# Graph attention on one core: one gathered tile in six steps, row by row through SyncE

## The chip, the cores and the metric

One NeuronCore of one Trainium2 chip. The metric is the device time of one execution in microseconds: 1808.31 us as the median of three runs before the change (1808.1 to 1808.62).

Engine names are those of the profile: PE (TensorE matmuls) and PEld (its weight loads), DVE (VectorE), ACT (ScalarE), POOL (GpSimd), SP (SyncE, which here only issues DMAs). A name with a q (SPq, POOLq) is that engine's instruction queue.

## What is computed

One layer of attention over a graph of 6250 nodes with 64 channels (4 heads of 16) and 206250 edges that are sorted by destination. For every edge: a score per head from the source's key, the destination's query and the edge's own projected values; then the sum of the sources' values, weighted by the scores, at each destination; then a residual and a layer norm.

```python
Qh, Kh, Vh = x @ Wq.T + bq, x @ Wk.T + bk, x @ Wv.T + bv      # each as (n, 4, 16)
Ee = edge_attr @ We.T + be
score = (Kh[src] * Qh[dst] * (1 / sqrt(16)) * Ee).sum(-1)
score = exp(clip(score, -5, 5))
msg = Vh[src] * score[..., None]
wV = segment_sum(msg, dst, num_segments=n)
out = layernorm(x + wV)
```

## The kernel before

**Preparation.** Keys and values of all nodes are computed once and written to a table in HBM, `kv_tab`, one row of 128 floats (512 B) per node; queries go to `q3_tab`. All sources and destinations lie in SBUF as `src_i` and `dst_i`, one column per tile.

**Tiles, groups, steps.** The edges are cut into 1612 tiles of 128 edges, 8 tiles make a group, and 2 groups a step; the last eight groups are steps of their own, 105 steps in all (`NS`). The loop over steps at L671 is unrolled in the program and its order is written by hand: each engine runs its instructions in the order in which that loop calls them, and waits for others by semaphores.

**Keys and values of an edge's source** come in two ways.
- `gather_kv` (L389): GpSimd issues one indirect DMA per tile (L391), which fetches 128 rows of `kv_tab` into one column of the step's buffer. There are `KVB = 5` such buffers (`kvs`, 128 x 16 x 128 floats), and `gather(s + 4)` (L507, called at L704) is issued in step s, so gathers may run up to four steps ahead.
- For the last two tiles of a step, in steps 6 to 96, the row of x is picked on TensorE by one-hot matrices that VectorE makes (`sources`, `hots` L470, `picks` L480), and keys and values are computed from it (`picked_kv`, L499), whereupon ScalarE writes them to the last two columns of the buffer. So in these steps GpSimd gathers 14 tiles of 16.

**A step's chain.** VectorE multiplies keys, queries and edge values (`products`: L565 waits for the step's gathers, then L566), sums by head (L572), ScalarE takes the exponential (L575), VectorE makes the message (L582); ScalarE and TensorE split it into three bf16 parts (L585, L593, L595), and TensorE sums by destination (L601). Interleaved with these are the next step's edge values (`edges`, L377 and L380), its queries (L558), and one-hot rows (ScalarE L535, L540).

**SP's queue.** In the order of the loop SP issues: the edges of two steps ahead (`fetch_edges`, L157, 512 KB), the two query windows of two steps ahead (`fetch_queries`, L171; their start rows come from registers that L165 loads from SBUF, 8 at a time), and at the end of some steps rows of x for a closed block (`close`, L636) and finished rows of the output (`norm`, L654). SP works in order and stops at a transfer whose buffer isn't free yet: L157 and L171 wait for TensorE to be done with the buffer's last use, L636 and L654 for VectorE. The built program counts the completion of SP's DMAs on eight semaphores in turn, so a DMA also waits, where that is not yet known to be past, for the one issued eight before it.

Of the kernel before, what the change touches and what calls it, by code (L numbers as in the profile page):

```python
# [7 lines left out]
F32 = mybir.dt.float32  # L8
BF16 = mybir.dt.bfloat16
I32 = mybir.dt.int32  # L10
AF = mybir.ActivationFunctionType
# [3 lines left out]
P = 128  # L15
N = 6250
C = 64
# [3 lines left out]
T = -(-E // P)  # L21
G = 8
NG = -(-T // G)

STEPS = [(g, 2) for g in range(0, NG - 8, 2)] + [(g, 1) for g in range(NG - 8, NG)]
NS = len(STEPS)
# [12 lines left out]
KVB = 5  # L39
# [10 lines left out]
def tiles_of(g):  # L50
    return min(G, T - g * G)
# [6 lines left out]
def groups_of(s):  # L58
    return range(STEPS[s][0], STEPS[s][0] + STEPS[s][1])
# [7 lines left out]
def picks_in(s):  # L67
    return M0 <= s <= LAST


def about_where(g):
    return STEP * g + g // 32

# [16 lines left out]

@with_exitstack
def tile_gnn(ctx: ExitStack, tc: tile.TileContext, x, xT, wT, bias, beT, weT, eT, src, dst, dst_rows,
             out):
    nc = tc.nc
    consts = ctx.enter_context(tc.tile_pool(name="consts", bufs=1))
    dram = ctx.enter_context(tc.tile_pool(name="dram", bufs=1, space=bass.MemoryType.DRAM))
# [3 lines left out]
    kv_tab = dram.tile([NR, 2 * C], F32, name="kv_tab")  # L100
# [6 lines left out]
    kvs = [consts.tile([P, 2 * G, 2 * C], F32, name=f"kv{i}") for i in range(KVB)]  # L107

    def kv_of(g):

        s = max(s for s in range(NS) if STEPS[s][0] <= g)
        j = (g - STEPS[s][0]) * G
        return kvs[s % KVB][:, j:j + G, :]
# [39 lines left out]
    def fetch_edges(q):  # L153

        lo, hi = q * LG * G // 2, min((q + 1) * LG * G, T) // 2
        et = loads.tile([P, LG * G // 2, P], F32, name="et")
        nc.sync.dma_start(et[:, :hi - lo, :], eT[:, lo:hi, :])  # L157
        for g in range(q * LG, min((q + 1) * LG, NG)):
            ET[g] = et[:, (g % LG) * G // 2:(g % LG + 1) * G // 2, :]

    def fetch_queries(g):

        if g % RG == 0:
            for i in range(2):
                _, vs = nc.values_load_multi_w_load_instructions(  # L165
                    base[i:i + 1, g // 2:(g + RG) // 2], engines=[mybir.EngineType.SP], min_val=0,
                    max_val=N, skip_runtime_bounds_check_because="the least of some destinations")
                for k, v in enumerate(vs):
                    at[g + 2 * k + i] = v
        QW[g] = windows.tile([3 * W, C], BF16, name="qw")  # L170
        nc.sync.dma_start(QW[g], q3_tab[bass.ds(at[g], W), :].rearrange("n (i c) -> (n i) c", i=3))  # L171

    with tc.tile_pool(name="nodes", bufs=1) as nodes, \
# [23 lines left out]
        for i in range(NB // CB):  # L197
            s = slice(i * CB * P, (i + 1) * CB * P)
# [18 lines left out]
        for g in range(XG):  # L217
            for j in range(G):
                nc.gpsimd.indirect_dma_start(
                    out=XS[g][:, j, :], out_offset=None, in_=x[:, :],  # L220
# [138 lines left out]
        for g in range(XG):  # L359
            for h in range(2):  # L360
                tp = npsum.tile([P, 2, P], F32, name="tp", bufs=2)
                for u in range(2):
                    j = 4 * h + 2 * u
# [25 lines left out]
    def gather_kv(g, j):  # L389
        t = g * G + j  # L390
        nc.gpsimd.indirect_dma_start(  # L391
            out=kv_of(g)[:, j, :], out_offset=None, in_=kv_tab[:, :],
            in_offset=bass.IndirectOffsetOnAxis(ap=src_i[:, t:t + 1], axis=0))
# [7 lines left out]
    with tc.If(rv == 0) as branch:  # L401

        with tc.tile_pool(name="work", bufs=2) as work, \
# [45 lines left out]
            def sources(s, i):  # L449

                if picks_in(s):
                    FAR[s, i] = work.tile([P, P], BF16, name="far")
                    nc.scalar.activation(FAR[s, i], row50, AF.Identity,
                                         bias=src_f[:, s - M0, i:i + 1], scale=-1.0)

            def sources_turned(s, i):
                if picks_in(s):
                    nc.tensor.transpose(from_b[i], FAR.pop((s, i)), ident_b)  # L460
# [46 lines left out]
            def gather(s):  # L507
                for g in groups_of(s):
                    for j in range(tiles_of(g)):
                        if not picks_in(s - 2) or g == STEPS[s][0] or j < G - 2:  # L510
                            gather_kv(g, j)


            def spread(g):

                pb = psum.tile([P, G, P], F32, name="pb")
                for b in range(0, tiles_of(g), 4):
                    nc.tensor.matmul(pb[:, b:b + 4, :],  # L518
                                     ident_b[:NR2, g // 2:g // 2 + 1].to_broadcast([NR2, P]),
                                     key_rows[:, g % 2, b * P:(b + 4) * P], start=True, stop=True)  # L520
                return pb
# [8 lines left out]
            def onehot_rows(g, pb):  # L530

                n = tiles_of(g)
                TO[g] = work.tile([3 * W, G, P], BF16, name="to", bufs=4)

                nc.scalar.activation(TO[g][:, :n, :], pb[:3 * W, :n, :], AF.Square,  # L535
                                     bias=minus_row3[:3 * W])

            def onehot_rows_rest(g):
                n = tiles_of(g)
                nc.scalar.activation(TO[g][:, :n, :], TO[g][:, :n, :], AF.Relu, bias=one_p[:3 * W],  # L540
                                     scale=-1.0)
# [55 lines left out]
            def sums(s):  # L597
                n = tiles_in(s)
                PA[s] = pa
                for j in range(n):  # L600
                    nc.tensor.matmul(PA[s], OH[s][:, j, :], M3[s][:, j], start=j == 0, stop=j == n - 1)  # L601
# [45 lines left out]
            def scales(lo, hi):  # L647
                nc.vector.reciprocal(rstd[:, lo:hi], rstd[:, lo:hi])
# [22 lines left out]
            for s in range(NS):  # L671
                more = s + 1 < NS
                for g in groups_of(s):
                    if g % LG == 0 and g + 2 * LG < NG:
                        fetch_edges(g // LG + 2)
                if s + 2 < NS:
                    for g in groups_of(s + 2):
                        fetch_queries(g)
                nexts = list(groups_of(s + 1)) if more else []
                if more:  # L680
                    onehot_rows(nexts[0], spread(nexts[0]))
                    onehot_rows_rest(nexts[0])
                if s:
                    sums(s - 1)
                sources_turned(s, 1)
                sources_turned(s + 1, 0)
                if nexts[1:]:
                    onehot_rows(nexts[1], spread(nexts[1]))
                making = [b for b in range(s * 2 * TB, (s + 1) * 2 * TB, TB) if b < NB]
                if making:  # L690
                    rest = table_parts(making[0])
                prod = products(s)
                picked(s - 1)
                if more:
                    edges(s + 1, 0)
                picks(s, 0, 0)
                score = scores(s, prod)
                if nexts[1:]:
                    onehot_rows_rest(nexts[1])
                if s:  # L700
                    add(s - 1)
                msg = message(s, score)
                if s + KVB - 1 < NS:
                    gather(s + KVB - 1)  # L704
                picked_turned(s - 1)
                if nexts[1:]:
                    edges(s + 1, 1)
                minus(s, msg, 0)
                hots(s, 1, 0)
                picks(s, 0, 1)  # L710
                minus(s, msg, 1)
                picked_kv(s - 1)
                if not more:

                    close(B - 2)
                    spreads(B - 2)
                hots(s, 1, 1)
                picks(s, 1, 0)
                sources(s + 1, 1)
                sources(s + 2, 0)  # L720
                if more:
                    if nexts[0] * G % KEYS == 0:
                        keys(nexts[0] * G)
                    onehot_edges(s + 1)
                    queries(s + 1)
                picks(s, 1, 1)
                hots(s + 1, 0, 0)
                hots(s + 1, 0, 1)
                if more:

                    while closed < B - 2 and due[closed] <= s:
                        close(closed)
                        spreads(closed)
                        closed += 1
                    if closed in BATCHES and closed > scaled:
                        roots(scaled, closed)
                        scales(scaled, closed)
                        scaled = closed
                    for _ in range(3):
                        if normed < scaled:  # L740
                            norm(normed)
                            normed += 1
                for i, b in enumerate(making):
                    if i:
                        rest = table_parts(b)
                    table_parts_rest(b, rest)
# [175 lines left out]
```

## Time and profile before

The profiled execution took 1808.39 us; its span from the first to the last instruction is 1806.6 us.

| engine | busy us | share of the span | instructions |
|---|---|---|---|
| PE | 1641.5 | 91% | 15751 |
| PEld | 1370.4 | 76% | 15751 |
| DVE | 1481.7 | 82% | 1695 |
| ACT | 912.0 | 50% | 1313 |
| POOL | 1351.8 | 75% | 1442 |

SP is not in this table, since instructions that issue DMAs are not counted as busy. The mean granted TensorE clock was 0.95. The DMA queues:

| queue | packets | MB | share of 16 engines |
|---|---|---|---|
| software_dynamic (GpSimd's) | 45760 | 92.76 | 19.6% |
| hardware_dynamic (SP's) | 60204 | 70.01 | 13.5% |

How to read the lines that follow in the prediction:
- A *group* line gives source line, engine, operation, out<-in and the number of instructions; after the bar busy time in us and the mean of one in ns; after the second bar the idle time of the engine just before them, and what ended most of it. "issue" means that the profile shows nothing that the engine waited for.
- A line of the *list of waits* gives who waited, for whom, us in total, how many times, and the longest.
- A line of the *timeline* gives start, duration, engine, source line, operation and shapes, and in brackets the idle time before it and what ended it. A line of the *chain* (the work that ended last, followed back from the end) gives start, duration and what.
- The *view of a source line* gives for each kind of instruction the count, the least, median and greatest duration in ns, and the first and last start.

### The profile page before, as it was taken

The page shows a single profiled execution, that of the slowest core. Times are in us where ns is not written, and L with a number is a line of the kernel's source. Part 1 is how long each engine was busy: PE and PEld are TensorE (multiplying, and loading weights), DVE is VectorE, ACT ScalarE, POOL GpSimd, SP SyncE. Part 2 cuts the span into 40 slices and gives each one's busy share as a digit, 9 for nine tenths or more (in the row PEclk, how much of TensorE's full clock was granted, in tenths as well). Part 3 has the DMA queues.
Part 4 walks back from the last instruction along what each step waited for, and adds up shares of the span by engine and source line. Part 5 has one row for each costly group of instructions (what it writes and reads, how often), then busy time and mean ns, then how long its engine had stood idle before and what let it go on. Part 6 is the DMA issues. An engine that isn't in the chain of part 4 may idle for free.

```text
span 1806.6 us, 38129 instructions
## 1 busy us (share of the span) xinstructions
PE 1641.5 (91%) x15751; PEld 1370.4 (76%) x15751; DVE 1481.7 (82%) x1695; ACT 912.0 (50%) x1313; POOL 1351.8 (75%) x1442
## 2 busy tenths in 40 slices
PE   8979999999999998999899898989999999999864
PEld 8547888888877777777777787877777778777632
DVE  6459999999988898888888888888988888888554
ACT  4465555555545454544545444455444545445443
POOL 7777777777777777777777777777777777777774
PEclk9968999999999999999999999999999999999855
DMA  8343323333323333332333323323332332332331
GB/s 239 112 120 92 92 80 104 80 101 83 92 79 93 91 84 90 99 81 81 92 91 90 80 79 93 91 79 98 84 92 80 92 91 79 91 91 79 89 79 45
DMA packets 106532, 166.30 MB, mean 92 GB/s; under 512 B 67501, under 2 KB 67822, under 8 KB 106236
## 3 DMA queue, kind: packets, MB, share of 16 engines
q0 software_dynamic: 45760, 92.76, 19.6%
q1 hardware_dynamic: 60204, 70.01, 13.5%
q8 instruction: 125, 2.05, 0.5%
q10 hardware_dynamic: 384, 1.00, 0.3%
q14 instruction: 59, 0.48, 0.1%
HBM read 156.32 MB, written 7.33 MB: 91 GB/s over the span
## 4 chain that ended last, share of the span: by engine, by line
PE 31%; POOL 28%; DVE 19%; issue 14%; DMA 4%; ACT 3%; DVEq 0%; SPq 0%; POOLq 0%; ACTq 0%
POOL kv L391 28%; PE pick L480 15%; DVE hot L470 7%; PE pe L380 4%; DMA kv<-kv_tab,src_i 4%; PE pq L593 2%; DVE prod L565 2%; DVE prod L566 2%; PE small L601 2%; DVE pq L582 2%; DVE small L572 2%; PE pb L518 2%; DVE acc L615 1%; PE pb L504 1%; PE pe L377 1%
## 5 line engine op out<-in xcount | busy, mean ns | idle before, releaser
L391 POOL DMA_INDIRECT kv<-kv_tab,src_i x1398 | 1319.7, 944 | 426.1 <-issue 403.5
L480 PE MATMUL pick<-parts,hot 128*128 128x192 bf16 x9100 | 825.6, 249 | 0.0
L480 PEld LDWEIGHTS <-hot 128*128 128x128 bf16 x9100 | 769.6, 99 | 38.0
L470 DVE TENSOR_TENSOR hot<-small,block 128x3200 bf16<-128x3200 bf16 x364 | 645.9, 1816 | 0.8 <-PE pick L480 0.8
L535 ACT ACTIVATE to<-pb,minus_row 126x1024 bf16<-126x1024 f32 x202 | 222.8, 1103 | 372.7 <-PE pb L518 368.7
L380 PEld LDWEIGHTS pe<-we_sb,et 128*128 128x128 f32 x1612 | 213.2, 206 | 152.9 <-issue 136.8
L595 ACT ACTIVATE msg<-pq 128x1024 bf16<-128x1024 f32 (+2 forms) x210 | 207.8, 990 | 219.7 <-PE pq L593 219.7
L565 DVE TENSOR_TENSOR prod<-kv,pq 128x1024 f32<-128x1024 f32 (+2 forms) x105 | 123.6, 1177 | 191.7 <-DMA kv<-kv_tab,src_i 92.7
L380 PE MATMUL pe<-we_sb,et 128*128 128x128 f32 x1612 | 254.3, 305 | 0.0
L540 ACT ACTIVATE to<-to,one_p 126x1024 bf16<-126x1024 bf16 x202 | 230.6, 1142 | 3.5
L377 PE MATMUL pe<-be_p,ones_b 3*128 3x512 bf16 x202 | 80.0, 396 | 104.8 <-DVE prod L566 104.8
L601 PEld LDWEIGHTS <-of 128*128 128x128 bf16 x1612 | 145.1, 102 | 30.9 <-issue 7.8
L601 PE MATMUL small<-msg,of 128*128 128x192 bf16 x1612 | 161.5, 256 | 0.5 <-ACT msg L595 0.5
L593 PE MATMUL pq<-msg,minus_b 128*128 128x512 bf16 x404 | 128.1, 396 | 30.8 <-ACT msg L585 16.6
L585 ACT ACTIVATE msg<-pq 128x1024 bf16<-128x1024 f32 (+2 forms) x105 | 103.9, 990 | 96.9 <-DVE pq L582 96.9
L572 DVE TENSOR_REDUCE small<-prod 128x64 f32<-128x1024 f32 (+2 forms) x105 | 123.6, 1177 | 13.3 <-PE small L460 7.5
L518 PE MATMUL pb<-key_rows,ident_b 112*128 112x512 bf16 x403 | 127.7, 399 | 2.8 <-ACT to L535 2.8
L566 DVE TENSOR_TENSOR prod<-prod,pe 128x1024 f32<-128x1024 f32 (+2 forms) x105 | 123.6, 1177 | 3.6
L582 DVE TENSOR_TENSOR pq<-kv,small 128x1024 f32<-128x1024 f32 (+2 forms) x105 | 123.5, 1176 | 1.4 <-ACT small L575 1.4
L548 DVE TENSOR_TENSOR of<-small,key 128x2048 bf16<-128x2048 bf16 (+2 forms) x105 | 123.2, 1173 | 0.3
L575 ACT ACTIVATE small<-small 128x64 f32<-128x64 f32 (+2 forms) x105 | 21.7, 207 | 131.0 <-DVE small L574 130.5
L558 PEld LDWEIGHTS <-to 126*128 126x128 bf16 x1612 | 63.5, 101 | 25.1 <-issue 24.9
(128 smaller groups left out, 992.1 us busy)
## 6 DMA issues: line engine op xcount, KB each, us to landing
et<-in_eT SPq DMA_DIRECT2D x100, 512.0 KB
kv<-kv_tab,src_i POOLq DMA_INDIRECT x1398
qw<-q_tab SPq DMA_DIRECT2D x202, 15.8 KB
kv_tab<-kv_sb SPq DMA_DIRECT2D x5, 640.0 KB
q_tab<-q SPq DMA_DIRECT2D x5, 480.0 KB
acc<-in_x SPq DMA_DIRECT2D x48, 32.0 KB
out<-y SPq DMA_DIRECT2D x48, 32.0 KB
raw<-in_x SPq DMA_DIRECT2D x6, 250.0 KB
```

Source lines behind the costliest of these rows:

```text
L380: nc.tensor.matmul(pe[:, 2 * u:2 * u + 2, :], et[:, u, :], we_sb, start=False, stop=u == n // 2 - 1, skip_group_check=True)
L391: nc.gpsimd.indirect_dma_start(out=kv_of(g)[:, j, :], out_offset=None, in_=kv_tab[:, :], in_offset=bass.IndirectOffsetOnAxis(ap=src_i[:, t ...
L470: nc.vector.tensor_tensor(HOT[s, i, h].rearrange("p b (a c) -> p b a c", c=2), pairs(from_b[i])[:, None].to_broadcast(shape), block2[:, bl ...
L480: nc.tensor.matmul(rows3[:, i], hot[:, k, :], parts[:, b], start=b == 0, stop=b == NB - 1)
L518: nc.tensor.matmul(pb[:, b:b + 4, :], ident_b[:NR2, g // 2:g // 2 + 1].to_broadcast([NR2, P]), key_rows[:, g % 2, b * P:(b + 4) * P], star ...
L535: nc.scalar.activation(TO[g][:, :n, :], pb[:3 * W, :n, :], AF.Square, bias=minus_row3[:3 * W])
L540: nc.scalar.activation(TO[g][:, :n, :], TO[g][:, :n, :], AF.Relu, bias=one_p[:3 * W], scale=-1.0)
L565: nc.vector.tensor_mul(prod[:, :n, :], kvs[s % KVB][:, :n, :C], PQ[s][:, :n, :])
L566: nc.vector.tensor_mul(prod[:, :n, :], prod[:, :n, :], PE[s][:, :n, :])
L593: nc.tensor.matmul(msg[:, lo:hi, :], minus_b, M3[s][:, lo:hi, i, :], start=False, stop=True, skip_group_check=True)
L595: nc.scalar.activation(M3[s][:, :n, i + 1, :], msg[:, :n, :], AF.Copy)
L601: nc.tensor.matmul(PA[s], OH[s][:, j, :], M3[s][:, j], start=j == 0, stop=j == n - 1)
```

## The change

Fifteen steps (12, 18, ..., 96) are "rowed": in each of them the gather of the tile in column 13 is left out of GpSimd's stream. In its place, SP fetches that tile's 128 rows of `kv_tab` one by one, 512 B each, into one partition after the other of a new tile `rk`. The source of each row is in a register; the registers are loaded eight at a time from `rs`, the tile's 128 sources as one row in SBUF, which SP fetches from a new input `src_rows` (the sources, a row of 128 per tile). The fetches are spread over SP's part of six steps, from eight to three steps before the rowed step: 16, 24, 24, 16, 24 and 24 rows, in the loop right behind the query windows. One step ahead of the rowed step, ScalarE copies `rk` to column 13 of the step's buffer, behind `sources` and ahead of `queries` in the loop. `rs` and `rk` have two buffers each.

```diff
+ROWED = 6
+ROWS = 8
+COLUMN = 2 * G - 3
+
+def is_rowed(s):
+    return s % ROWED == 0 and 2 * ROWED <= s < NS - 8
...
             def gather(s):
                 for g in groups_of(s):
                     for j in range(tiles_of(g)):
+                        if is_rowed(s) and (g - STEPS[s][0]) * G + j == COLUMN:
+                            continue
                         if not picks_in(s - 2) or g == STEPS[s][0] or j < G - 2:
                             gather_kv(g, j)
+
+            RS, RK = {}, {}
+
+            def fetch_rows(s):
+                to = -(-(s + 3) // ROWED) * ROWED
+                k = s - (to - 2 - ROWED)
+                if not is_rowed(to):
+                    return
+                if k == 0:
+                    RS[to] = work.tile([1, P], I32, name="rs")
+                    t = STEPS[to][0] * G + COLUMN
+                    nc.sync.dma_start(RS[to], src_rows[t:t + 1, :])
+                    RK[to] = work.tile([P, 2 * C], F32, name="rk")
+                for lo in range(k * P // ROWED // ROWS * ROWS, (k + 1) * P // ROWED // ROWS * ROWS, ROWS):
+                    _, vs = nc.values_load_multi_w_load_instructions(
+                        RS[to][:, lo:lo + ROWS], engines=[mybir.EngineType.SP], min_val=0, max_val=N,
+                        skip_runtime_bounds_check_because="sources are nodes")
+                    for i, v in enumerate(vs):
+                        nc.sync.dma_start(RK[to][lo + i:lo + i + 1, :], kv_tab[bass.ds(v, 1), :])
+
+            def rows_fetched(s):
+                if is_rowed(s):
+                    nc.scalar.activation(kvs[s % KVB][:, COLUMN, :], RK.pop(s), AF.Copy)
...
                 if s + 2 < NS:
                     for g in groups_of(s + 2):
                         fetch_queries(g)
+                fetch_rows(s)
                 nexts = list(groups_of(s + 1)) if more else []
...
                 sources(s + 1, 1)
                 sources(s + 2, 0)
+                if s + 1 < NS:
+                    rows_fetched(s + 1)
                 if more:
...
+        "in_src_rows": padded(src, P * T).reshape(T, P),
```

More of the change, by code (lines that the diff above doesn't have):

```diff
@@ L92, in tile_gnn @@
 def tile_gnn(ctx: ExitStack, tc: tile.TileContext, x, xT, wT, bias, beT, weT, eT, src, dst, dst_rows,
-             out):
+             src_rows, out):
     nc = tc.nc
```

## The prediction

> **What bounds the kernel now.** I first read the page's table of busy time. It does not settle the question: PE is at 91%, VectorE (DVE) at 82%, GpSimd (POOL) at 75%. So the second view is the page's costliest groups, for POOL's one big line, and the third the list of who waited for whom, POOL's part.
>
> ```profile
> L391 POOL DMA_INDIRECT kv<-kv_tab,src_i x1398 | 1319.7, 944 | 426.1 <-issue 403.5
> ```
>
> ```profile
> POOL kv L391 <- issue: 403.5, 1324, 0.3
> ```
>
> A gather of one 128-row tile is busy for 0.944 us, and before 1324 of 1398 of them POOL stood idle for 0.30 us with nothing to wait for. The other rows of that list are each a few times 0.3 us too: the same gap under another name. No gather ever waited for a buffer. Busy and gap together, 1319.7 + 426.1 = 1745.8 us over 1398, are 1.249 us per gather, and the timeline agrees: the first kv gather starts at 43.13 us, the last at 1787.68, and 1744.55 / 1397 = 1.2488. So POOL, "75% busy", is one unbroken stream from 43 us until 19 us before the end. The end of the chain of work shows what follows:
>
> ```profile
> 1782.38 0.31 issue
> 1782.69 2.46 DMA kv<-kv_tab,src_i
> 1785.15 0.03 DVEq L565
> 1785.18 0.05 issue
> 1785.23 0.05 DVEq L565
> 1785.28 0.04 issue
> 1785.33 0.70 DVE prod L565
> ```
>
> The products of a step start as soon as its last gather has landed, 2.46 us after that gather began.
>
> Is the stream the bound all along, or are the other engines as slow? That is read from the starts of `prod` (L565), one per step, in VectorE's timeline: steps 18, 20, then 48, 50.
>
> ```profile
> 364.70 1.22 DVE L565 TENSOR_TENSOR prod<-kv,pq 128x1024 f32<-128x1024 f32 x1 [0.29 <-issue]
> 396.09 1.22 DVE L565 TENSOR_TENSOR prod<-kv,pq 128x1024 f32<-128x1024 f32 x1 [0.29 <-issue]
> ...
> 876.46 1.22 DVE L565 TENSOR_TENSOR prod<-kv,pq 128x1024 f32<-128x1024 f32 x1 [2.65 <-PE pb L518]
> 911.38 1.22 DVE L565 TENSOR_TENSOR prod<-kv,pq 128x1024 f32<-128x1024 f32 x1 [2.81 <-DMA kv<-kv_tab,src_i]
> ```
>
> Steps 18 to 20 take 31.39 us, 15.70 a step: there the gathers are ahead and only PE, VectorE and ScalarE set the pace. Steps 48 to 50 take 34.92 us, 17.46 a step, with 2.7 us of idling ahead of `prod`. Fourteen gathers at 1.2488 are 17.48. Counting gathers by step in POOL's timeline gives the lead of step s's last gather over its `prod`: 36.98 us at step 6, 15.50 at step 18, 3.51 at step 24, and from there to the end between 2.57 and 4.99. So until about step 24 (450 us) the compute loop catches up on the gathers, and from then on POOL alone sets the time. (The wait ahead of step 48's `prod` bears PE's name, but the last gather of that step began at 873.68 and lands 2.5 us later: it ended last too.)
>
> **Part 1: what is removed.** In the 15 steps 12, 18, ..., 96 one of 14 gathers goes. POOL waits for nothing, so its stream shortens by 15 x 1.2488 = 18.7 us, and so does the start of the last gather (1787.68 to 1768.95); the 19 us behind it hold no changed work. Can the compute loop follow? A six-step period falls from 6 x 17.48 = 104.9 to 103.6 us, 17.27 a step against 15.70: 9.4 us to spare in six steps. All 18.7 us arrive, though steps before 24 are not bound by POOL: the catching up only ends slightly later.
>
> **Part 2: what is added on SP.** Per rowed step there are 128 row fetches of 512 B, 16 register loads of 8 sources, and one load of the sources. The order of the built program gives each row fetch two register instructions, one wait (for the DMA issued eight earlier on SP's queue) and the DMA: the same form as the existing `qw` fetch. The view of line 171:
>
> ```profile
> L171 SPq FUSED_REGOPS  x202: 37/37/51, 54.9 to 1772.1; - x101
> L171 SPq MOVE qw<-q_tab x202: 29/29/38, 55.8 to 1772.2; - x101
> L171 SPq DMA_DIRECT2D qw<-q_tab x202: 321/352/1417, 55.9 to 1772.2; - x101
> L171 SPq EVENT_SEMAPHORE  x185: 17/17/28, 55.0 to 1772.1; - x185
> ```
>
> The medians sum to 37 + 29 + 352 + 17 = 0.435 us a row. The register load is line 165's:
>
> ```profile
> L165 SPq TENSOR_LOAD <-base x26: 525/708/1097, 52.9 to 1671.8; - x26
> ```
>
> Per six steps SP needs 128 x 0.435 = 55.7, 16 x 0.708 = 11.3, about 2.9 for the load of sources and its landing (0.36 + the 2.5 us that a gather takes to land), and what it does today: per step one `et` (0.36), two `qw` (0.88) and half an `acc` and an `out` row (0.36), 9.7 with the loads of `base`: 79.6 us of 103.6. SP fits, at 77%. In a step with 24 rows it is 10.4 + 2.1 + 1.6 = 14.1 us of 17.27.
>
> The row price is the unknown. Below: 0.245 us, the shortest `acc` DMA, + 0.083 = 0.33. Above: the one-partition load `w_sb<-in_bias` took 0.457 us to issue, at start-up, so 0.54 with its registers; and its landing took 4.01 us, which with eight in flight caps the rate at 0.50 a row. Even 0.54 makes 93 us of 103.6. I take 0.435, the row of the same instruction in the same stage. Up to (103.6 - 23.9) / 128 = 0.62 us a row nothing is lost.
>
> Here a rule speaks against the change. The Trainium skill, "DMA: Bandwidth & Descriptors", section "Rules for kernel authors", says to merge small transfers since under 64 KB one pays mostly overhead, and its "Anatomy of one DMA" puts the fixed cost near 2.0 us (fitted on the GpSimd path). One after another, 128 x 2.0 + 23.9 = 280 us per period: 15 x (280 - 104.9), over 2.6 ms lost. But the same section calls that mostly completion latency. What a queue pays is its issue time if several are in flight, and the eight here make it 2.0 / 8 = 0.25 a row, under the 0.435 of issuing. I go by the row.
>
> What is queued behind the rows on SP: the next step's `et` and `qw`, `acc` and `out`. SP also stops at `acc` and `out` for VectorE's close at a step's end (L636 waited 385.8 us for it in 23 places), so at worst it begins a step together with the engines. Its `et` is then needed a step later, `qw` nearly two; 14 us of rows leave both on time. Rows for a step are issued 8 to 3 steps ahead and copied one step ahead, two steps to spare. Cost: nothing; without that cover it is the first rival.
>
> **Part 3: the copy.** 15 copies of 128x128 on ScalarE. Nearest row: L455, 128x128 from f32, 0.401 us, which makes 6.0 us in all. They stand right behind L455, where ScalarE then idles (3.99 us ahead of L535 at 910.62), so they cost nothing. If the rows were late, ScalarE's L535, L540 and thus PE's `queries` would stand behind that wait. `prod` now also waits for ScalarE, one step early.
>
> **Part 4: contention.** The rows add 1920 x 512 B = 1.0 MB to 166 MB, and many small pieces to engines that are about 33% busy. Does SP's traffic stretch the gathers' spacing? In POOL's timeline after 100 us, 1039 intervals with no SP issue average 1.2487 us, 134 with a `qw` 1.2484, 62 with an `et` 1.2479. I take zero. Later landing of gathers by some tenths (2.97 us instead of 2.46 once beside an `et`) delays each step alike and does not add up.
>
> Sum: 1808.39 (the profiled execution, span 1806.6 with 1.8 around it; the median of the runs is 0.08 lower) - 18.7 = **1789.6 us**.
>
> **The rivals.**
> 1. *SP becomes the bound: slower.* Place: the row fetch. It decides from 0.62 us a row. For it: the four `qw` at 55.88 us took 3.10 us, 0.78 each (they also waited there); single `et` issues took 0.83 us. At 0.78, 124 us a period, so 15 x (124 - 104.9) = +287 us, 2095 us; at 0.65, 107.1 a period and +33 us. Against: 0.435 in the median, and a form not seen here only in its single partition. Chance 0.13.
> 2. *Contention: part of the gain.* 1383 gathers stretched by 13.5 ns each eat it all. The averages above show no such stretch, but no burst of 24 small DMAs is in this trace. With half of it: 1799 us. Chance 0.08, nearly all of it still faster.
> 3. *Nothing moves* (the loop needs 17.4 us a step whatever POOL does, or a new wait takes the place): 1808. The 15.70 us of steps 18 to 20 speak against it. Chance 0.02.
> 4. My forecast, 1789.6: 0.77, with 1787.5 to 1793 as its own range (the gap between gathers could also shrink or grow by a few ns).
>
> **The numbers.** The range 1787 to 1797 takes in the forecast and the better half of rival 2; left out are the slow case and the rest, below 2 in 10. Faster by over 0.2% (3.6 us, about what a measurement of this kernel can tell from no change) 0.84, within it 0.03, slower 0.13.
>
> **What would show it.** Right: 1383 gathers, still 1.249 us apart; the last starts near 1769 us; row fetches at 0.33 to 0.54 us each; no wait of ScalarE ahead of the copy; lead over `prod` still 2.5 to 5 us from about step 25. Wrong: rows above 0.62 us, with SP issuing without a pause, ScalarE waiting for `rk`, and steps of about 20 us; or a gather spacing above 1.255 us.

## The result, and the profile after

The changed kernel takes 1790.03 us (median of four runs, 1789.78 to 1790.19) against 1808.46 us before: a ratio of 0.9899, interval 0.9887 to 0.991. Its profiled execution took 1789.88 us with a span of 1788.0 us, 18.5 and 18.6 us less than before.

These times, and those of the two light kernels below, come from chips on which the kernel before takes 1808 us; the ten other experiments ran on four chips on which it takes 3014 to 3119 us, with engines pausing between instructions for no wait that the profile shows, so each of those is compared with the kernel before on its own chip alone.

GpSimd's stream in the changed kernel: first the group of gathers on the page, then POOL's row of the list of waits, then the last two gathers in its timeline.

```profile
L402 POOL DMA_INDIRECT kv<-kv_tab,src_i x1383 | 1305.3, 944 | 421.7 <-issue 399.8
```

```profile
POOL kv L402 <- issue: 399.8, 1311, 0.3
```

```profile
1767.60 0.94 POOL L402 DMA_INDIRECT kv<-kv_tab,src_i  x1 [0.30 <-issue]
1768.85 0.94 POOL L402 DMA_INDIRECT kv<-kv_tab,src_i  x1 [0.30 <-issue]
```

Fifteen gathers fewer, each as long as before, with the same 0.30 us ahead of it. The stream begins at 43.04 us (43.13 before), and (1768.85 - 43.04) / 1382 is 1.2488 us a gather, unchanged to the fourth digit. The last gather starts 18.83 us earlier: 18.73 for the fifteen gathers and 0.09 for the earlier start. The stretch behind it, to the end of the span, is 19.2 us against 18.9, so 18.6 us of it arrive. The share of POOL on the page is still 75%.

The starts of `prod` in VectorE's timeline, for steps 18 and 20, then 36 and 54:

```profile
365.30 1.22 DVE L602 TENSOR_TENSOR prod<-kv,pq 128x1024 f32<-128x1024 f32 x1 [0.29 <-DMA kv<-kv_tab,src_i]
396.69 1.22 DVE L602 TENSOR_TENSOR prod<-kv,pq 128x1024 f32<-128x1024 f32 x1 [0.29 <-DMA kv<-kv_tab,src_i]
...
660.35 1.22 DVE L602 TENSOR_TENSOR prod<-kv,pq 128x1024 f32<-128x1024 f32 x1 [1.17 <-PE pick L491]
971.26 1.22 DVE L602 TENSOR_TENSOR prod<-kv,pq 128x1024 f32<-128x1024 f32 x1 [0.55 <-DMA kv<-kv_tab,src_i]
```

Early steps still take 15.70 us (31.39 for two): they have not become faster, they only stay that fast for longer. (The wait ahead of step 36's `prod` bears PE's name, but the last gather of that step began 2.89 us ahead of it.) From step 36 to 54 it is 310.91 / 18 = 17.27 us a step, the 103.6 us for six that 83 gathers take.

What SP does with its new work: the view of the rows' line, of ScalarE's copy, and a stretch of SP's timeline.

```profile
L544 SPq FUSED_REGOPS  x1920: 37/37/42, 150.2 to 1655.1; - x192
L544 SPq MOVE rk<-kv_tab x1920: 29/29/29, 150.3 to 1655.2; - x192
L544 SPq DMA_DIRECT2D rk<-kv_tab x1920: 224/228/286, 150.4 to 1655.3; - x192
```

```profile
L548 ACT ACTIVATE kv<-rk x15: 305/306/309, 267.9 to 1694.1; 128x128 f32<-128x128 f32 x15
```

```profile
895.81 0.37 SPq L168 DMA_DIRECT2D et<-in_eT  x1
901.87 0.89 SPq L182 DMA_DIRECT2D qw<-q_tab  x2
903.79 11.82 SPq L544 DMA_DIRECT2D rk<-kv_tab  x24
918.51 0.37 SPq L673 DMA_DIRECT2D acc<-in_x  x1
```

A step's 24 rows take 11.82 us, and SP still comes to the next `acc` with 2.9 us to wait for VectorE. SP's longest wait before the change, at `acc`, and the same wait after it:

```profile
SPq L636 <- DVE acc L634: 385.8, 23, 18.4
```

```profile
SPq L673 <- DVE acc L671: 107.2, 23, 10.3
```

It fell from 385.8 to 107.2 us in as many places, and the wait at `et` for PE's edge values from 385.5 to 58.1. The rows have filled time in which SP stood still. PE's list does name the rows, 25.7 us in 20 places ahead of its edge values (L391), but its weight loads there stood idle for 133.4 us in all, against 152.9 before.

### The profile page after: what moved, and what is told of

It reads as the page before. It is cut to its first block, busy times and chain, and to the rows that moved or that the text cites. A ratio compares the mean times of both kernels' runs of the same rounds, so it can differ in the third digit from the quotient of the medians.

```text
span 1788.0 us, 44286 instructions
## 1 busy us (share of the span) xinstructions
PE 1638.5 (92%) x15751; PEld 1369.6 (77%) x15751; DVE 1481.6 (83%) x1695; ACT 914.0 (51%) x1328; POOL 1337.4 (75%) x1427
## 3 DMA queue, kind: packets, MB, share of 16 engines
q1 hardware_dynamic: 64074, 71.01, 14.1%
q8 instruction: 125, 2.05, 0.5%
## 4 chain that ended last, share of the span: by engine, by line
PE 38%; POOL 29%; issue 14%; DVE 13%; DMA 4%; ACT 3%; DVEq 0%; SPq 0%; POOLq 0%; ACTq 0%
POOL kv L402 29%; PE pick L491 18%; PE pe L391 5%; DVE hot L481 5%; DMA kv<-kv_tab,src_i 3%; PE pq L630 2%; PE small L638 2%; DVE prod L603 2%; DVE prod L602 2%; PE pb L555 2%; PE pe L388 2%; PE pb L515 1%; PE pq L595 1%; DVE pq L619 1%; PE ps L350 1%
## 5 line engine op out<-in xcount | busy, mean ns | idle before, releaser
L402 POOL DMA_INDIRECT kv<-kv_tab,src_i x1383 | 1305.3, 944 | 421.7 <-issue 399.8
L391 PEld LDWEIGHTS pe<-we_sb,et 128*128 128x128 f32 x1612 | 209.7, 203 | 133.4 <-issue 95.3
L391 PE MATMUL pe<-we_sb,et 128*128 128x128 f32 x1612 | 250.3, 302 | 0.0
L595 PEld LDWEIGHTS <-to 126*128 126x128 bf16 x1612 | 63.5, 101 | 25.3 <-issue 25.1
```

Of the source, the lines that this page charges most:

```text
L391: nc.tensor.matmul(pe[:, 2 * u:2 * u + 2, :], et[:, u, :], we_sb, start=False, stop=u == n // 2 - 1, skip_group_check=True)
L402: nc.gpsimd.indirect_dma_start(out=kv_of(g)[:, j, :], out_offset=None, in_=kv_tab[:, :], in_offset=bass.IndirectOffsetOnAxis(ap=src_i[:, t ...
```

## The experiments

Two theories. T: GpSimd's stream alone sets the time from about step 25 on, a gather is worth its 1.249 us, and rows and copies are hidden while SP is not full. The rivals: the rows cost something that the gain hides (contention, lateness), or SP is nearly full already.

**Leaving out matmuls: is it GpSimd's stream?** Both kernels, with one of 25 matmuls left in each chain of picks.

```diff
-                    for k in range(NB // 2):
+                    for k in (h * (NB // 2 - 1),):
                         b = h * NB // 2 + k
```

> The kernel before, with one of 25 matmuls left in each chain of picks (9100 become 364, so the picked rows are not summed whole). On the chips of the runs so far PE stands idle[...] and holds the kernel at 3000 us; with about 40% of its instructions left, GpSimd's stream should hold it again. Theory: the gathers run 1.249 us apart once the first steps are past, with no wait of POOL for VectorE there, and the time is 1830 to 1900 us (the stream starts later than 43 us on these chips). Rival (these chips are slow for another reason): still far above 2000 us.

> The changed kernel with the same matmuls left out. Theory (15 gathers leave a stream that sets the time, and the rows cost nothing): 18.7 us less than its pair before, 17.5 at least if the stream is held up at the very start. Rival (the gain needs the picks, or rows cost where PE's instructions are fetched slowly): less than 10 us, or a loss.

They ran on a chip on which the kernel before takes 1808.18 us, so the first expectation's guess of 1830 to 1900, made for the other chips, does not apply. Measured: 1808.42 us for the light kernel before (ratio 1.0, 0.9991 to 1.001), 1789.84 us for the light changed kernel (0.9897, 0.9881 to 0.9914). The groups of the gathers, light kernel before and light changed kernel:

```profile
L391 POOL DMA_INDIRECT kv<-kv_tab,src_i x1398 | 1319.5, 944 | 426.0 <-issue 391.6
```

```profile
L402 POOL DMA_INDIRECT kv<-kv_tab,src_i x1383 | 1305.4, 944 | 421.7 <-issue 383.5
```

PE's busy time fell from 1641.5 to 1232.8 us (91% to 68%), although its granted clock fell too (0.95 to 0.74), and the time moved by 0.24 us in 1808, within the interval: the busiest engine by the page is not the bound, and the picks' matmuls lie wholly behind GpSimd's stream. The change is worth 18.6 us without them and 18.4 with them. T holds. And since 15 gathers are 18.73 us, what 1920 rows, 240 register loads and 15 copies add comes to about 0.15 us, within the spread of the runs. By the interval of the ratio alone a cost of some 3 us could hide; the gathers' spacing, 1.2488 us with and without rows, leaves no place for one in the stream, and at its end the traces show 0.3 us. The gathers left out without rows, which would test this directly, were not run on such a chip.

**Gathers without rows, rows without gathers.** The first leaves out the 15 gathers and puts nothing in their place; the second keeps all gathers and adds the rows.

```diff
-                fetch_rows(s)
...
-                if s + 1 < NS:
-                    rows_fetched(s + 1)
```

```diff
-                        if is_rowed(s) and (g - STEPS[s][0]) * G + j == COLUMN:
-                            continue
...
-                    nc.scalar.activation(kvs[s % KVB][:, COLUMN, :], RK.pop(s), AF.Copy)
+                    nc.scalar.activation(work.tile([P, 2 * C], F32, name="spare_kv"), RK.pop(s), AF.Copy)
```

> Leaves out the 15 gathers and everything that replaces them: no row fetches, no copy (column 13 of a rowed step holds old rows). Theory (GpSimd's stream sets the time, SP's rows and ScalarE's copy are hidden): the same time as the changed kernel, 1790 us within 1 us, last gather at 1769 us. Rival (the rows cost something that the 18.7 us hide, by contention for the DMA engines or by late copies): faster than the changed kernel, 1785 or less.

> Keeps all 1398 gathers and adds the row fetches; ScalarE copies them to a tile that nobody reads. Theory: the time of the kernel before, 1808.4 us within 1 us, gathers still 1.249 us apart. Rival (contention): slower, 1811 us or more, with the spacing of the gathers above 1.250 us.

> The first four runs fell on a chip on which the kernel before itself took 3108 us, with PE idle[...] and GpSimd waiting for VectorE: they can't tell these theories apart, which speak of a kernel that GpSimd's stream holds. So the same kernel again: it leaves out the 15 gathers, and also the row fetches and copies that replace them. Theory (rows and copies are hidden): within 1 us of the changed kernel, 1790 us where the kernel before takes 1808. Rival (they cost something that the 18.7 us hide): 1785 us or less.

> Keeps all 1398 gathers and adds the 1920 row fetches; ScalarE copies them to a tile that nobody reads. Where the kernel before takes about 1808 us: theory (rows are hidden beside GpSimd's stream) within 1 us of the kernel before, gathers 1.249 us apart; rival (contention for DMA engines) 1811 us or more, spacing above 1.250 us. Where the kernel before takes about 3000 us[...]: the rows cost again about 1%, since GpSimd's stream then hides nothing.

All four fell on chips where the kernel before takes 3108 us (the first two), 3021 and 3014 us. Gathers left out: 3080.83 us (ratio 0.9905, 0.9889 to 0.9921) and 2992.55 us (0.9903, 0.9885 to 0.9921). Rows added: 3137.7 us (1.0094, 1.008 to 1.0108) and 3096.17 us (1.0281, 1.0261 to 1.0301). What bounds there is seen in the second run with rows: POOL's two longest waits, then PE's.

```profile
POOL kv L402 <- DVE pq L617: 1241.8, 98, 14.4
POOL kv L402 <- issue: 383.6, 1239, 4.4
```

```profile
PE pq L593 <- issue: 585.9, 467, 4.8
PE pick L491 <- issue: 258.5, 360, 1.9
```

GpSimd stands 1241.8 us waiting for VectorE to free buffers (in the kernel before on a chip with 1808 us it waited for nobody), and PE pauses over 800 us ahead of single matmuls, waiting for nothing that is shown. These runs cannot decide between the theories as they were put. They show something else: where GpSimd's stream is not the bound, the rows cost 30 and 82 us (0.9% and 2.8%; about 1% was expected of the second), and leaving out the gathers brings 27 and 29. The changed kernel as a whole was not run on such a chip; that it would gain nothing there, or lose, is argued from these sums, not shown.

**More rowed steps: one in five, one in four** (there `ROWED = 4`).

```diff
-ROWED = 6
+ROWED = 5
```

> One rowed step in five: 18 gathers less than the kernel before instead of 15. In the changed kernel's trace SP's rows take about 69 us of a period (rows 0.42 us apart, 16 register loads of 0.78, the load of the sources 2.3) and its old work 1.6 us a step, so SP needs 69 + 8 = 77 us of the 86 that five steps take. Theory: SP still fits, 1808.4 - 18 x 1.249 = 1785.9 us. Rival (SP in truth is nearly full at one in six, since it also stops at each close): rows late, no gain over 1790 us.

> The whole kernel with one rowed step in five, 18 gathers less than before the change. Theory (SP needs 77 of 86 us): where the kernel before takes 1808 us, 1785.9 us, 3.7 less than the changed kernel. Rival (SP, which also stops at each close, is too late with the rows): 1790 us or more, with ScalarE waiting ahead of the copy.

> One rowed step in four: 23 gathers less. SP needs 69 + 6.4 = 75.4 us for four steps, and GpSimd's stream 68.7. Theory: SP is now the bound, 18.9 us a step, which makes about 1808 + 84 x 1.4 = 1925 us, 1900 to 1970; SP issues nearly without a pause, and ScalarE waits ahead of the copy. Rival (rows are cheaper than counted or SP's old work overlaps): 1808.4 - 23 x 1.249 = 1779.7 us.

On chips with 3108 and 3119 us before: one in five takes 3148.73 us (1.0129, 1.0113 to 1.0145) and 3148.86 us (1.0102, 1.0081 to 1.0124), one in four 3230.76 us (1.0401, 1.0382 to 1.042). More rows, more time, as with the rows alone; ScalarE has no wait ahead of the copy in any of the three. Whether one in five is the faster kernel where GpSimd bounds stays open: its 1785.9 us was not measured.

**One in four with few matmuls: SP as the bound.**

> One rowed step in four, with one of 25 pick matmuls left (the picked rows are not summed whole), so that only GpSimd's stream and SP's queue can hold it. GpSimd's stream would need 68.7 us for four steps, SP 75.4 (69 us for the rows, loads and sources, 1.6 a step for its old work). Theory: SP is now the bound, 18.9 us a step, 1950 us (1900 to 1970), and GpSimd waits for VectorE to free buffers. Rival (SP has more room than counted): 1808.4 - 23 x 1.249 = 1779.7 us.

3040.96 us, on a chip with 3118.63 before. Far above the forecast of 1950, but on a chip for which that was not made; the mechanism is there. The longest of PE's waits, then the view of the row's line:

```profile
PE pe L391 <- DMA et<-in_eT: 666.2, 87, 12.8
```

```profile
L544 SPq MOVE rk<-kv_tab x2944: 1/29/1398, 200.2 to 2937.7; - x197
L544 SPq DMA_DIRECT2D rk<-kv_tab x2944: 2/228/1422, 200.9 to 2937.7; - x197
```

PE waits 666 us for edges, which stand on SP's queue behind the rows; SP issues from 1501 to 1620 us of its timeline almost without a gap, and waits for VectorE or PE hardly anywhere. So SP's queue is what mostly holds this kernel, and the place where it hurts is `et`, which the prediction's Part 2 names as queued behind the rows; ScalarE, which the first rival saw waiting for `rk`, has no wait ahead of the copy. The price is not the one of the changed kernel, though: 32 rows take 25.16 us instead of some 16. Most rows are 0.41 us apart here too, but for 14 us in one stretch (1514.95 to 1528.93) they come 1.2 to 2.1 us apart, with a row's move and DMA drawn out to 1.4 us. That an undisturbed SP is full at one in four is thus not shown.

**One row at a time: what a fetch costs when nothing overlaps.** Rows of a group go to the same partition, so that seven of eight wait for the one before (the tile is then wrong, VectorE first fills it with zeros, and one of 25 pick matmuls is left).

```diff
+                    nc.vector.memset(RK[to], 0.0)
...
-                        nc.sync.dma_start(RK[to][lo + i:lo + i + 1, :], kv_tab[bass.ds(v, 1), :])
+                        nc.sync.dma_start(RK[to][lo:lo + 1, :], kv_tab[bass.ds(v, 1), :])
```

> One rowed step in six as in the changed kernel, but the eight rows of a group go to the same partition, so that seven of eight fetches wait until the one before has landed (the rowed tile is wrong, and one of 25 pick matmuls is left). The load of the sources waited 1.98 us for its landing in the changed kernel. Theory (the changed kernel pays the issue, 0.42 us a row, since eight are in flight; one at a time each would pay its landing): a row takes 2.2 to 2.4 us, a period 112 x 2.3 + 16 x 0.42 + 25 = 289 us, and the kernel some 4600 us. Rival (a row's landing is short, or the order on the queue costs nothing): a row under 1 us, the time below 2400 us.

3220.76 us, on the same chip: neither the 4600 of the theory nor below the 2400 of the rival. The longest of PE's waits shows that the edges now come late behind the rows:

```profile
PE pe L391 <- DMA et<-in_eT: 1404.2, 88, 23.7
```

So the order on the queue costs a lot, but a row far less than expected. Four rows in a row in SP's timeline of this kernel, and then three of the light changed kernel (on its own chip):

```profile
1507.75 0.23 SPq L545 DMA_DIRECT2D rk<-kv_tab  x1
1508.94 0.23 SPq L545 DMA_DIRECT2D rk<-kv_tab  x1
1510.13 0.23 SPq L545 DMA_DIRECT2D rk<-kv_tab  x1
1511.31 0.23 SPq L545 DMA_DIRECT2D rk<-kv_tab  x1
```

```profile
905.62 0.23 SPq L544 DMA_DIRECT2D rk<-kv_tab  x1
906.03 0.23 SPq L544 DMA_DIRECT2D rk<-kv_tab  x1
906.44 0.23 SPq L544 DMA_DIRECT2D rk<-kv_tab  x1
```

One at a time, a row takes 1.19 us (1.22 in the median of all); with eight in flight 0.41. Those 0.41 us are SP's own pace: eight in flight would allow 1.19 / 8 = 0.15, and in the changed kernel no row's DMA lasts longer than 0.286 us. I had expected 2.2 to 2.4 us from the 1.98 us that SP waits for the load of sources, a transfer of the same 512 B; why that one lands later is not shown (it stands right behind two `qw` on the queue). At 1.19 us SP would need 112 x 1.19 + 16 x 0.41 + 25 = 165 us of a period's 103.6 (an estimate; 25 us are the loads and SP's old work): without the overlap the change would be a heavy loss where GpSimd sets the time. That was not run there.

**Twelve gathers a step.** The gathers of columns 12 and 13 are left out in steps 12 to 96 with nothing in their place, to find the pace of the other engines.

> Leaves out the gathers of columns 12 and 13 in steps 12 to 96 with nothing in their place (old rows are used). GpSimd then needs 12 x 1.249 = 15.0 us a step. Theory: the other engines' 15.7 us a step, read from steps 18 to 20 of the kernel before, become the bound; prod of step 96 starts near 270.5 + 84 x 15.70 = 1589 us, and the whole takes about 1677 us (1660 to 1695); GpSimd waits for VectorE to free buffers. Rival (the other engines need 17 us a step whatever GpSimd does): about 1790 us. Other rival (GpSimd's stream stays the bound): 1808 - 169 x 1.249 = 1597 us.

2843.09 us against 3118.63 (0.9117, 0.9095 to 0.9138), on a chip where PE pauses as above (639.9 us ahead of L595 alone). The edit takes out 170 gathers, not the 169 of the expectation. The floor of 15.70 us a step cannot be read from it; it rests on the early steps of the two traces, where it shows twice.

## Why the prediction was right

- *The bound.* Forecast: 18.7 us, the last gather at 1768.95 us, 1789.6 us in all. Measured: 1768.85 us, and 1789.88 in the profiled execution, 1790.03 in the median. The mechanism is the one forecast: the stream has no wait for another engine before or after, and taking 409 us of busy time off PE moves nothing.
- *The row's price.* Forecast 0.435 us, measured 0.41 us from start to start, but not for the reason given. Issuing the DMA takes 0.228 us, not the 0.352 of a `qw`; the durations of a row add up to 37 + 29 + 228 = 0.294 us, and 0.12 us between them is in no duration at all. The wait that the forecast counted for every row stands as an instruction of its own ahead of only 13 of 1920. Two errors nearly cancelled: the nearest row was dearer, and a sum of durations leaves out the gaps between instructions. That the price came out near was luck; that SP had room did not hang on it, since the gain held up to 0.62 us by the forecast's own sum.
- *SP's sum.* Forecast 79.6 us of a period, which leaves out about 1 us of the `base` loads (26 x 0.708 us in the whole kernel): six steps of old work at 1.6 us are 9.6 of its 9.7 already. From 885.03 to 985.09 us SP's timeline has six steps, with waits of 5.7, 2.9 and 8.6 us at `qw` and `acc`: 83 us of work, 80%. A register load costs more than forecast (0.781 us, and 1.24 us from row to row across it).
- *The copy.* 0.306 us against 0.401 forecast; no engine's list of waits has a row for it, and ScalarE has none ahead of it.
- *Contention.* Spacing of the gathers 1.2488 us before and after; forecast zero, measured zero.
- *Catching up.* Forecast: the lead of the gathers over `prod` settles at about step 25. It was 5.14 us at step 26 and 2.92 at step 28, some three steps later than I thought. Behind that, single steps reach 5.76 us (step 63), above the forecast 5 us; before the change the greatest is 5.05 (the last step), where the prediction read at most 4.99. Nothing follows from them, since GpSimd waits for nobody.
- *The rivals.* SP as the bound did not come about at one in six; its mechanism showed at one in four on a chip with a stretched row price, and its threshold of 0.62 us a row was not measured. The Trainium skill's fixed cost of about 2.0 us for a DMA ("DMA: Bandwidth & Descriptors", "Anatomy of one DMA") was fitted on GpSimd's path, and rows on SP stay below it: 1.19 us for a row that waits for its forerunner, and 0.41 us in the queue. The load of sources comes near it, with waits of 1.98 us on average and 2.6 at most. Deciding by issue time instead of the estimate of 280 us a period from that figure was right, and it was right because of the eight in flight: one at a time, even 1.19 us a row would not fit.

## What to carry to other kernels

Look for the engine that never waits, not for the one with the highest share: here a stream of equal instructions with a constant gap and no releaser was the bound at 75% busy, and one instruction less in it was worth its whole spacing while the other engines had room (15.70 us a step against 17.27). Work could be moved off it at a high price (1920 small transfers for 15 gathers) because the engine that took it stood still otherwise, several of its transfers were in flight, and its queue was not full. Where GpSimd's stream does not set the time the move can lose: on the chips with 3000 us one rowed step in five cost 1.0 and 1.3%. Price a transfer on a queue by the distance from start to start, not by its duration or by its landing, and add up the queue per period against the period's length.

## What the runs showed of the hardware

- A row's fetch makes two packets on the hardware queue: from 60204 to 64074 on the page is 3870, and 2 x (1920 rows + 15 loads of sources) is 3870. By their sizes in the traces 1935 of the new packets have 512 B and 1935 have 4 B: a one-partition transfer of 512 B goes out whole, with one packet of 4 B beside it.
- On four chips the same kernel takes 3014 to 3119 us. In their traces single instructions of PE or SP follow each other 0.7 to 3 us apart for stretches of some 10 to 14 us, with no wait shown, while GpSimd's gathers keep their 0.944 to 0.946 us. PE's pauses with no wait shown sum to 715 to 907 us there with all matmuls, and to 243 and 55 us in the light kernels. It looks as if instructions arrive too slowly, but no run here shows the cause, and the queue that carries instructions shows nothing of it: 125 packets and 2.05 MB in both, for 0.5% of 1806.6 us in the kernel before and 0.3% of 3080.4 us on such a chip with the gathers left out. The granted clock is lower there (0.77 to 0.81 with all matmuls, against 0.95), but that alone does not make the time: the light kernels took 1808 and 1790 us at 0.74 to 0.76.
- On those chips each gather left out was worth 1.8 and 1.9 us (27.2 and 28.7 us for 15) and 1.6 us (275.5 for 170), more than its 1.249 us on GpSimd, though GpSimd waited for others over 1100 us. So there it isn't GpSimd's time that a gather costs; what it is stays open.
